# A transformer block's first FFN layer by seven half products: GpSimd's add moved behind the last product, a Relu moved one step later, and the residual rows added in the second pair step

## The chip, the cores and the metric

The kernel runs on one core of one Trainium2 chip. The time is the device time of an execution in microseconds (us); for the kernel before it is the median of three runs. The engines are called PE (TensorE: matmuls, into PSUM), DVE (VectorE), ACT (ScalarE), POOL (GpSimd) and SP (SyncE, which only issues DMAs here). Each engine works through its own queue of instructions in order.

## The reference, cut to what matters

Eight sequences (batches) of 1024 rows with 256 features go through one block: normalise, self-attention, gated residual, normalise, a two-layer FFN with Relu, gated residual. All is float32.

```python
h = _layernorm(x, axis=-1) * (1 + ca) + sa
x = x + ga * _L0_attn_ref(h, L0_attn_w_lhs, L0_attn_w_rhs)   # softmax(lhs @ rhs^T) @ h
h = _layernorm(x, axis=-1) * (1 + cb) + sb
x = x + gb * _L0_ffn_ref(h, L0_ffn_W1, L0_ffn_b1, L0_ffn_W2, L0_ffn_b2)

def _L0_ffn_ref(hidden_states, W1, b1, W2, b2):
    h = jax.nn.relu(jnp.einsum('bsh,hi->bsi', hidden_states, W1) + b1)    # 256 -> 1024
    return jnp.einsum('bsi,ih->bsh', h, W2) + b2                          # 1024 -> 256
```

## The kernel before, in words

**Steps.** A batch b has eight steps i, one for each tile of 128 rows of its attention. A step makes the scores of the row tile two steps ahead (`direct`, L372: PE, then a copy by ACT to SBUF), the maximum of a row (`row_max`), its subtraction (`subtract`, L439, DVE), the exponent (`exponent`, L451, ACT) and the product of weights and values (`product`, L456: 16 matmuls of 257 columns on PE; then `product_out` on DVE). Scores are symmetric in their shape: `mirror` (L393) makes the other half by a block transpose on DVE and a trip through DRAM on SP's queue.

**The FFN of an earlier half batch runs in the same steps.** A half batch (group g, 512 rows) of batch b-1 needs four steps: in the first two (i = 0, 1 for one group, 4, 5 for the other; the code's `first`) the first layer, two *pairs* of 128 hidden columns each, so pairs c = 0, 1 in step 0 or 4 and c = 2, 3 in step 1 or 5. In the other two the second layer: `y_first` (L655) and `y_second` (L677).

**A pair.** `pair_products` (L581) and `pair_last` (L625) make the columns c and c+4 for both 256-row halves with seven half-size products in place of eight, and sums around them. Six products go to the PSUM tiles pa, pb and pc; ACT copies pa to `kept` (L598). `pair_sums` (L607) then adds: DVE's L611 and L614 make `u`, POOL's L617 adds the second half of `kept` to both parts of `u` and writes the second halves of both column blocks of f, DVE's L620 and L623 write the first halves. `pair_last` issues the seventh product into pa, and DVE's L630 adds it to what POOL wrote. `pair_relu` (L632) applies the Relu on ACT (L634, L635) and `pair_turn` (L639) makes the sums ft that the second layer reads (POOL, L644 to L647; `ft[:, 1]`, called ft1 here, by L645).

**The second layer** takes f (both blocks, all four pairs) in ya and yb, then ft1 and ft0 in the second halves of ya and yb, then the rest in `y_second`. Its result goes through a transpose in DRAM; the read comes back as Y behind a mirror's read on SP's queue (`read_back`). `y_add` (L716, POOL's L721, two instructions of 512 elements) adds it to x, and `y_out` stores x.

**Buffers.** Four PSUM tiles (`ps_a`) serve pa, pb, pc, the attention's product and ya to yd; two (`ps_s`) serve the scores. `kept` has two buffers, Y, f and ft have one each.

**Order.** Instructions stay in the order in which the program writes them, engine by engine (`pin`, L61). The main loop's body (L988 to L1136) is that order. In a pair step it reads: products of the first pair, its sums, the turn of the pair before, mirror, last product, subtract, products of the second pair, Relu of the first, exponent, sums of the second, turn of the first, `y_add` (in steps 0 and 4, by `back`), row_max, last product and Relu of the second. After that come `subtract(extra)`, `turns` (in step 5 `prepare_turn`, L319, which makes lT on DVE, L335, and rT on ACT, L339, for the next batch's scores), `norms` (in step 1 a memset and a power on POOL, in step 5 a power), the last turn, and the attention's product. Behind the loop the last batch's FFN follows without attention, with a plain second layer (`second`, L749).

Of the kernel before, what the change touches and what calls it, by code (L numbers as in the profile page):

```python
# [10 lines left out]
F32 = mybir.dt.float32  # L11
AF = mybir.ActivationFunctionType
ALU = mybir.AluOpType
# [3 lines left out]
P = 128  # L17
# [5 lines left out]
def adaln_block_kernel(  # L23
# [13 lines left out]
    nc = tc.nc  # L37
# [5 lines left out]
    HALF = 512  # L43
    TH = HALF // P
    H2 = HALF // 2
    NH = NI // 2
# [6 lines left out]
    work = ctx.enter_context(tc.tile_pool(name="work", bufs=3))  # L53
# [113 lines left out]
    b1_col = lambda i: cols[:, i : i + 1]  # L167
# [111 lines left out]
    def read_back():  # L279
        while reads:  # L280
            reads.pop(0)()
# [111 lines left out]
    def mirror(b, i):  # L393
        if i == NT - 1:
            return
        n = NT - 1 - i
        if b == 0:
            mirror_first(i)
            return
        T = two.tile([P, NV, NT * V], F32, tag="T", name=f"Tm_{b}_{i}")  # L400
        T = T.rearrange("p b m -> p (b m)")[:, : NV * n * V].rearrange(
            "p (b m) -> p b m", b=NV
        )
        nc.vector.transpose(  # L404
            T.rearrange("p b (j v) -> p b j v", v=V),
            sc_t[b][:, i + 1 :, :, i, :].rearrange("p j b v -> p b j v"),
        )
        move(
            sc_t[b][:, i, :, i + 1 :, :].rearrange("p a j v -> p a (j v)"), T, n * V,
            f"m{b}_{i}",  # L410
        )
# [39 lines left out]
    def exponent(b, i):  # L451
        nc.scalar.activation(pT_t[b, i], pT_t[b, i], AF.Exp)  # L452
# [122 lines left out]
    lo, hi = slice(0, H2), slice(H2, HALF)  # L575
    pairs = {}

    def mm(out, lhsT, rhs):
        nc.tensor.matmul(out, lhsT=lhsT, rhs=rhs, start=True, stop=True)  # L579

    def pair_products(b, g, c, between=None):  # L581

        if c == 0:
            ffn["f"] = two.tile([P, NI, HALF], F32, tag="f", name=f"f_{b}_{g}", bufs=1)
            if b < B - 1:
                ffn["ft"] = two.tile([P, 3, NH, H2], F32, tag="ft", name=f"ft_{b}_{g}", bufs=1)
        hT, hs = ffn["hT", g]
        n = ts(c, P)
        s1, a22 = (w1[:, k, ds((c + NH) * P, P)] for k in range(2))

        pool, tag = (ps_s, "s") if b == B - 1 else (ps_a, "a")
        pa = ps_a.tile([P, HALF], F32, tag="a", name=f"pa_{b}_{g}_{c}")
        pb = pool.tile([P, HALF], F32, tag=tag, name=f"pb_{b}_{g}_{c}")
        pc = ps_a.tile([P, HALF], F32, tag="a", name=f"pc_{b}_{g}_{c}")
        mm(pa[:, lo], w1[:, 0, n], hT[:, 0, lo])
        mm(pa[:, hi], s1, hs[:, 0])
        kept = work.tile([P, HALF], F32, tag="kept", name=f"kept_{b}_{g}_{c}", bufs=2)
        nc.scalar.copy(kept, pa)  # L598
        if between:
            between()  # L600
        mm(pb[:, lo], w1s[:, 0, n], hs[:, 1])
        mm(pb[:, hi], w1s[:, 1, n], hs[:, 2])
        mm(pc[:, lo], w1[:, 1, n], hT[:, 1, lo])
        mm(pc[:, hi], a22, hT[:, 0, hi])
        pairs[c] = pa, pb, pc, kept

    def pair_sums(b, g, c):  # L607
        pa, pb, pc, kept = pairs[c]
        f = ffn["f"]
        u = work.tile([P, 2, H2], F32, tag="u", name=f"u_{b}_{g}_{c}", bufs=2)  # L610
        nc.vector.scalar_tensor_tensor(  # L611
            u[:, 0], pb[:, lo], b1_col(c), kept[:, lo], ALU.add, ALU.add
        )
        nc.vector.scalar_tensor_tensor(  # L614
            u[:, 1], pb[:, hi], b1_step[:, c : c + 1], u[:, 0], ALU.add, ALU.add
        )
        nc.gpsimd.tensor_tensor(  # L617
            f[:, c::NH, hi], u, kept[:, None, hi].to_broadcast([P, 2, H2]), ALU.add
        )
        nc.vector.scalar_tensor_tensor(  # L620
            f[:, c, lo], pc[:, lo], b1_col(c), kept[:, lo], ALU.add, ALU.add
        )
        nc.vector.tensor_tensor(f[:, c + NH, lo], pc[:, hi], u[:, 1], ALU.add)  # L623

    def pair_last(b, g, c):  # L625

        pa = pairs.pop(c)[0]
        f = ffn["f"]
        mm(pa[:, lo], w1s[:, 2, ts(c, P)], ffn["hT", g][0][:, 1, hi])
        nc.vector.tensor_tensor(f[:, c, hi], pa[:, lo], f[:, c, hi], ALU.add)  # L630

    def pair_relu(c):  # L632
        f = ffn["f"]
        nc.scalar.activation(f[:, c, :], f[:, c, :], AF.Relu)  # L634
        nc.scalar.activation(f[:, c + NH, :], f[:, c + NH, :], AF.Relu)  # L635
# [3 lines left out]
    def pair_turn(c):  # L639


        f, ft = ffn["f"], ffn["ft"]
        add = nc.gpsimd.tensor_tensor
        add(ft[:, 0, c], f[:, c + NH, hi], f[:, c, hi], ALU.subtract)  # L644
        add(ft[:, 1, c], ft[:, 0, c], f[:, c, lo], ALU.add)  # L645
        add(ft[:, 2, c], ft[:, 1, c], f[:, c + NH, lo], ALU.subtract)
        add(f[:, c, hi], f[:, c, hi], f[:, c, lo], ALU.subtract)  # L647
# [68 lines left out]
    def y_add(b, g, q):  # L716

        read_back()
        x2 = x_t[b, g][:, ts(q, 2), :].rearrange("p t (h b u) -> p (t h) b u", h=2, u=V)
        y = ffn["rows", b, g].rearrange("p t h b u -> p (t h) b u")[:, ts(q, 4)]  # L720
        nc.gpsimd.tensor_tensor(x2, x2, y, ALU.add)  # L721
# [100 lines left out]
    b1_step = const.tile([P, NH], F32, name="b1_step")  # L822
# [105 lines left out]
    def turns(b, i):  # L928

        if b > 0 and i == 2:  # L930
            ffn_turn(b - 1, 1)
        if 0 < b < B - 1:
            if i == 3:
                prepare_turn(b + 1, 0)
            elif i == 5:
                prepare_turn(b + 1, 1)
        if i == (7 if b < B - 1 else 6):
            ffn_turn(b, 0)
# [45 lines left out]
    def weights(b, i):  # L984
        subtract(b, i)
        exponent(b, i)
# [3 lines left out]
    for b in range(B):  # L990
        for i in range(NT):
# [4 lines left out]
            fb, fg = b - 1, i // TH  # L996
            first = b > 0 and i % TH < 2
            c = i % TH * 2
# [48 lines left out]
            if first:  # L1047

                ub, ug = (b - 1, 0) if i >= TH else (b - 2, 1)
                back = i % TH == 0 and ub >= 0  # L1050
                pair_products(fb, fg, c, turn_max)
                if (b, i) == (1, 0):
                    weights(*late)
                    late = None
                pair_sums(fb, fg, c)
                if c > 0:
                    pair_turn(c - 1)
                if ahead:
                    mirror(*ahead)
                pair_last(fb, fg, c)  # L1060
                if i == 4 and b + 1 < B:
                    prepare_blocks(b + 1, 1)
                    xg_times(b + 1, 1)
                if late:
                    subtract(*late)
                pair_products(fb, fg, c + 1, (lambda: max_turn(*extra)) if extra else None)
                pair_relu(c)
                if late:
                    exponent(*late)
                middle(b, i)  # L1070
                pair_sums(fb, fg, c + 1)
                pair_turn(c)
                if back:
                    for q in range(2):
                        y_add(ub, ug, q)
                if ahead and ahead != extra:
                    row_max(*ahead)
                pair_last(fb, fg, c + 1)
                pair_relu(c + 1)
            else:  # L1080
                half = i % TH - 2
                if i == 3 and b + 1 < B:
                    prepare_stats(b + 1, 1)
                if not ahead:

                    product(b, i)
                    product_out(b, i)
                    if i == NT - 1:
                        ffn_stats(b, 1)
                (y_second if half else y_first)(fb, fg, turn_max)  # L1090
                if ahead:
                    mirror(*ahead)
                spare()
                early(b, i)
                if late:
                    weights(*late)
                middle(b, i)
                if i == 2 and b + 1 < B:
                    load_x(b + 1, 1)
                if i == 3 and b + 1 < B:  # L1100
                    prepare_norm(b + 1, 1)
                    x_plus(b + 1, 1)
                spare()
                if ahead:
                    row_max(*ahead)
                if half:
                    y_second_sums(fb)
                else:
                    y_first_sums()
                spare()  # L1110
            if extra:
                subtract(*extra)
            turns(b, i)
            norms(b, i)
            if extra:
                exponent(*extra)
# [24 lines left out]
    b = B - 1  # L1141
# [73 lines left out]
```

## Time and profile before

| what | value |
|---|---|
| three timed runs | 791.08, 792.75, 793.41 us; median 792.75 |
| the profiled execution's own time | 792.76 us |
| its span, first to last instruction | 790.9 us |
| mean granted clock of PE | 0.998 |
| POOL's longest waits | for DVE's L558 at L567 107.7 us in 15, for L614 at L617 101.3 us in 35 |
| ACT's waits at Relu L634 for DVE's L630 | 76.6 us in 56 |
| DVE's waits at L630 for POOL's L617 | 29.9 us in 28 |
| POOL's waits at L721 for the read of Y | 20.4 us in 8, the longest 8.4 |
| one batch in steady state | 94.0 us, for instance from 236.39 to 330.29 in step 5's product |

In a row of a timeline the first number is the start in us from the first instruction, the second the stretch that the row covers; then engine, line, operation, output and inputs, and the count of instructions. A bracket at the end is the idle time of the engine before it, and what ended that. In a row of the list of waits the numbers are the total in us, how often, and the longest. Idle time of an engine other than PE costs nothing by itself.

### The profile page before, as it was taken

Reading aid. Unit: us, or ns where it says so; the run is one execution under the profiler, and the core shown is the slowest. Engines: PE = TensorE matmul, PEld = TensorE weight load, DVE = VectorE, ACT = ScalarE, POOL = GpSimd, SP = SyncE. Lnnn points to the kernel's source line nnn. Section 1 sums busy time; section 2 is a strip of 40 time slices with the busy share of each in tenths; the row PEclk is TensorE's granted clock in tenths of the full one; section 3 lists DMA queues with packets and bytes.
Section 4 is the critical chain, followed back from the end, with each engine's and each line's share of the span. In section 5 each row is a group of like instructions: output and inputs, shape, how many; then the busy total and the mean of one; then the engine's idle time right before and its main releaser. Section 6 shows DMA issues by size and latency. Waiting matters only on the chain.

```text
span 790.9 us, 10632 instructions
## 1 busy us (share of the span) xinstructions
PE 771.9 (98%) x3374; PEld 619.8 (78%) x3374; DVE 564.2 (71%) x1212; ACT 346.9 (44%) x581; POOL 461.6 (58%) x573
## 2 busy tenths in 40 slices
PE   8999999999999999999999998999999999999997
PEld 4676888778887888778887886878888778888886
DVE  6696889658786778857888567885789658574632
ACT  4463535425444454435445344452535425242511
POOL 1365665927657385745759347493665927357631
PEclk9999999999999999999999999999999999999999
DMA  5323344355444354344533544335444345142220
GB/s 188 121 74 116 109 123 126 104 143 166 121 111 135 111 170 132 115 144 119 157 97 110 172 122 126 98 114 172 129 148 120 96 126 166 34 123 85 80 81 27
DMA packets 106192, 95.14 MB, mean 120 GB/s; under 512 B 29684, under 2 KB 98832, under 8 KB 106136
## 3 DMA queue, kind: packets, MB, share of 16 engines
q1 hardware_dynamic: 98392, 85.81, 36.6%
q10 hardware_dynamic: 7744, 8.65, 3.7%
q8 instruction: 27, 0.44, 0.2%
q14 instruction: 29, 0.24, 0.1%
HBM read 50.62 MB, written 43.81 MB: 119 GB/s over the span
## 4 chain that ended last, share of the span: by engine, by line
PE 72%; DVE 10%; POOL 9%; issue 5%; ACT 2%; DMA 1%; SPq 0%; DVEq 0%; POOLq 0%
PE po L464 20%; PE psc L381 13%; PE yc L651 6%; PE ya L651 6%; PE yb L651 6%; PE pa L579 6%; POOL f L617 5%; PE pb L579 4%; PE pc L579 3%; PE yd L651 3%; DVE pT L443 2%; POOL x L721 2%; PE py L756 2%; DVE u L614 2%; DVE u L611 1%
## 5 line engine op out<-in xcount | busy, mean ns | idle before, releaser
L464 PE MATMUL po<-xg,pT 128*128 128x257 f32 x1024 | 235.6, 383 | 5.2 <-DVE f L630 5.2
L464 PEld LDWEIGHTS po<-xg,pT 128*128 128x128 f32 x1024 | 194.4, 191 | 36.4 <-DVE f L630 8.4
L617 POOL TENSOR_TENSOR f<-u,kept 128x512 f32<-128x512 f32 x64 | 81.3, 1271 | 101.5 <-DVE u L614 101.3
L381 PE MATMUL psc<-rT,lT 128*128 128x512 f32 (+3 forms) x384 | 135.9, 488 | 3.9 <-ACT rT L339 3.9
L388 ACT COPY sc<-psc 128x512 f32<-128x512 f32 (+3 forms) x96 | 45.2, 474 | 147.3 <-PE psc L381 147.3
L381 PEld LDWEIGHTS psc<-rT,lT 128*128 128x128 f32 x384 | 68.2, 190 | 44.7 <-issue 22.5
L452 ACT ACTIVATE pT<-pT 128x1024 f32<-128x1024 f32 x64 | 67.7, 1058 | 54.5 <-DVE pT L443 54.5
L443 DVE TENSOR_TENSOR pT<-sc,pm 128x1024 f32<-128x1024 f32 x64 | 77.2, 1207 | 16.7 <-PE pm L436 16.7
L431 DVE TENSOR_REDUCE m<-sc 128x1 f32<-128x1024 f32 x64 | 77.4, 1210 | 0.6
L598 ACT COPY kept<-pa 128x512 f32<-128x512 f32 x64 | 37.5, 585 | 87.0 <-PE pa L579 87.0
L567 POOL TENSOR_TENSOR hs<-hT 128x256 f32<-128x256 f32 x16 | 11.7, 730 | 107.7 <-DVE hT L558 107.7
L634 ACT ACTIVATE f<-f 128x512 f32<-128x512 f32 x64 | 40.5, 632 | 77.6 <-DVE f L630 76.6
L579 PE MATMUL pb<-hs,w1s 128*128 128x256 f32 x256 | 65.9, 380 | 0.7 <-POOL hs L569 0.7
L579 PE MATMUL pc<-hT,w 128*128 128x256 f32 x256 | 65.7, 379 | 0.0
L611 DVE SCALAR_TENSOR_TENSOR u<-pb,cols,kept 128x256 f32<-128x256 f32 x64 | 30.6, 479 | 40.0 <-PE pb L579 39.1
L579 PEld LDWEIGHTS pc<-hT,w 128*128 128x128 f32 x256 | 48.6, 190 | 6.6
L630 DVE TENSOR_TENSOR f<-pa,f 128x256 f32<-128x256 f32 x64 | 27.0, 421 | 36.5 <-POOL f L617 29.9
L495 POOL TENSOR_TENSOR x<-x,rows 128x256 f32<-128x256 f32 x64 | 45.5, 739 | 12.1 <-ACT rows L857 12.1
L579 PEld LDWEIGHTS pb<-hs,w1s 128*128 128x128 f32 x256 | 45.8, 190 | 8.6 <-POOL hs L569 1.1
L651 PE MATMUL yc<-f,w2s 128*128 128x256 f32 x224 | 52.1, 379 | 0.0
L651 PEld LDWEIGHTS yc<-f,w2s 128*128 128x128 f32 x224 | 41.5, 190 | 10.2 <-issue 2.9
L404 DVE STREAM_TRANSPOSE Tm<-sc 128x896 f32<-128x896 f32 (+6 forms) x49 | 34.7, 708 | 19.1 <-ACT sc L388 18.3
(135 smaller groups left out, 1411.2 us busy)
## 6 DMA issues: line engine op xcount, KB each, us to landing
D_f<-T_f SPq DMA_DIRECT2D x60, 128.0 KB, 2.8
X_f<-D_f SPq DMA_DIRECT2D x15, 512.0 KB, 3.5
D_a<-T_a SPq DMA_DIRECT2D x56, 128.0 KB, 3.3
D_y<-T_y SPq DMA_DIRECT2D x56, 128.0 KB, 2.3
Y<-D_y SPq DMA_DIRECT2D x14, 512.0 KB, 3.9
out_dram<-x SPq DMA_DIRECT2D x14, 512.0 KB, 4.0
X_a<-D_a SPq DMA_DIRECT2D x13, 512.0 KB, 3.2
x<-in_L_attn_x_dram ACTq DMA_DIRECT2D x12, 512.0 KB, 4.0
```

The costliest lines, as they stand in the source:

```text
L381: nc.tensor.matmul(psc[:, : hi - lo], lhsT=lT_t[b, i // TH][:, k, ts(i % TH, P)], rhs=rT_t[b, n][:, k, lo - n * HALF : HALF], start=(k == ...
L388: nc.scalar.copy(score_row(b, i)[:, lo // V : hi // V, :], psc[:, : hi - lo].rearrange("p (n v) -> p n v", v=V),)
L431: nc.vector.tensor_reduce(m, score_row(b, i), AX.XY, ALU.max)
L443: nc.vector.tensor_tensor(pT.rearrange("p j (a v) -> p j a v", v=V), score_columns(b, i), pm[:, :P].rearrange("p (j a v) -> p j a v", j=1, ...
L452: nc.scalar.activation(pT_t[b, i], pT_t[b, i], AF.Exp)
L464: nc.tensor.matmul(po[:, : D + 1], lhsT=pT[:, t, :], rhs=xg_t[b][:, t, 0 : D + 1], start=(t == 0), stop=(t == NT - 1),)
L495: queue.append(lambda: nc.gpsimd.tensor_tensor(out, in0, row, op))
L579: nc.tensor.matmul(out, lhsT=lhsT, rhs=rhs, start=True, stop=True)
L611: nc.vector.scalar_tensor_tensor(u[:, 0], pb[:, lo], b1_col(c), kept[:, lo], ALU.add, ALU.add)
L617: nc.gpsimd.tensor_tensor(f[:, c::NH, hi], u, kept[:, None, hi].to_broadcast([P, 2, H2]), ALU.add)
L634: nc.scalar.activation(f[:, c, :], f[:, c, :], AF.Relu)
L651: nc.tensor.matmul(out, lhsT=lhs(c), rhs=rhs(c), start=(c == 0), stop=(c == NH - 1))
```

## The change

In `pair_sums` DVE writes u (half as large) and, in place of its second part, the second half of block c+4 of f itself; POOL's add is gone from there. `pair_last` adds the seventh product to u and writes the second half of block c; POOL's add of `kept` follows it, in place on both blocks of f. `kept` gets a third buffer. In the main loop the Relu of a second pair moves from the end of steps 0 and 4 to behind the first products of steps 1 and 5; the turn of the pair before follows the last product instead of the sums; the second pair's last product comes ahead of `row_max` and of the first pair's turn. `y_add`, and with it `y_out`, moves from steps 0 and 4 to steps 1 and 5, between the turn of pair 1 and the last product of pair 3. In step 5 `turns` is called ahead of the last Relu instead of behind it. The code behind the loop is unchanged, but calls the changed functions.

```diff
-        kept = work.tile([P, HALF], F32, tag="kept", name=f"kept_{b}_{g}_{c}", bufs=2)
+        kept = work.tile([P, HALF], F32, tag="kept", name=f"kept_{b}_{g}_{c}", bufs=3)
...
     def pair_sums(b, g, c):
-        u = work.tile([P, 2, H2], F32, tag="u", name=f"u_{b}_{g}_{c}", bufs=2)
+        u = work.tile([P, H2], F32, tag="u", name=f"u_{b}_{g}_{c}", bufs=2)
+        pairs[c] = pa, kept, u
+        far = f[:, c + NH, hi]
         nc.vector.scalar_tensor_tensor(
-            u[:, 0], pb[:, lo], b1_col(c), kept[:, lo], ALU.add, ALU.add
+            u, pb[:, lo], b1_col(c), kept[:, lo], ALU.add, ALU.add
         )
         nc.vector.scalar_tensor_tensor(
-            u[:, 1], pb[:, hi], b1_step[:, c : c + 1], u[:, 0], ALU.add, ALU.add
-        )
-        nc.gpsimd.tensor_tensor(
-            f[:, c::NH, hi], u, kept[:, None, hi].to_broadcast([P, 2, H2]), ALU.add
+            far, pb[:, hi], b1_step[:, c : c + 1], u, ALU.add, ALU.add
         )
...
-        nc.vector.tensor_tensor(f[:, c + NH, lo], pc[:, hi], u[:, 1], ALU.add)
+        nc.vector.tensor_tensor(f[:, c + NH, lo], pc[:, hi], far, ALU.add)
...
     def pair_last(b, g, c):
-        pa = pairs.pop(c)[0]
+        pa, kept, u = pairs.pop(c)
         mm(pa[:, lo], w1s[:, 2, ts(c, P)], ffn["hT", g][0][:, 1, hi])
-        nc.vector.tensor_tensor(f[:, c, hi], pa[:, lo], f[:, c, hi], ALU.add)
+        nc.vector.tensor_tensor(f[:, c, hi], pa[:, lo], u, ALU.add)
+        nc.gpsimd.tensor_tensor(
+            f[:, c::NH, hi],
+            f[:, c::NH, hi],
+            kept[:, None, hi].to_broadcast([P, 2, H2]),
+            ALU.add,
+        )
...
-                back = i % TH == 0 and ub >= 0
+                back = i % TH == 1 and ub >= 0
                 pair_products(fb, fg, c, turn_max)
...
+                if c > 0:
+                    pair_relu(c - 1)
                 pair_sums(fb, fg, c)
-                if c > 0:
-                    pair_turn(c - 1)
                 if ahead:
                     mirror(*ahead)
                 pair_last(fb, fg, c)
+                if c > 0:
+                    pair_turn(c - 1)
+                if back:
+                    for q in range(2):
+                        y_add(ub, ug, q)
...
                 pair_sums(fb, fg, c + 1)
-                pair_turn(c)
-                if back:
-                    for q in range(2):
-                        y_add(ub, ug, q)
+                pair_last(fb, fg, c + 1)
                 if ahead and ahead != extra:
                     row_max(*ahead)
-                pair_last(fb, fg, c + 1)
-                pair_relu(c + 1)
+                pair_turn(c)
+                if i == 5:
+                    turns(b, i)
+                if c > 0:
+                    pair_relu(c + 1)
...
-            turns(b, i)
+            if i != 5:
+                turns(b, i)
```

## The prediction

> **What bounds the kernel now.** I read the page's busy times first, then the list of who waited for whom, cut to TensorE (PE), and then the timelines of single engines in the two places it points at. The page settles the kind of kernel:
>
> ```profile
> PE 771.9 (98%) x3374; PEld 619.8 (78%) x3374; DVE 564.2 (71%) x1212; ACT 346.9 (44%) x581; POOL 461.6 (58%) x573
> L617 POOL TENSOR_TENSOR f<-u,kept 128x512 f32<-128x512 f32 x64 | 81.3, 1271 | 101.5 <-DVE u L614 101.3
> ```
>
> PE is busy 98% of a 790.9 us span. The change adds and removes no matmul, so a time can change only through PE's pauses. In the list of waits those inside the loop have two names:
>
> ```profile
> PE po L464 <- DVE f L630: 5.2, 8, 2.6
> PE psc L381 <- ACT rT L339: 3.9, 6, 0.7
> ```
>
> The reader is to see that 8 and 6 are about one per batch (b = 1 to 7), plus one outlier of 2.6 us. The ends of matmuls are modelled, so I size the pauses from start to start, in the timeline of PE around step 5 of batch 3:
>
> ```profile
> 329.38 0.59 PE L579 MATMUL pa<-hT,w1s 128*128 128x256 f32 x2
> 330.29 3.73 PE L464 MATMUL po<-xg,pT 128*128 128x257 f32 x16 [0.32 <-DVE f L630]
> 333.86 1.88 PE L381 MATMUL psc<-rT,lT 128*128 128x512 f32 x4
> 336.39 1.98 PE L381 MATMUL psc<-rT,lT 128*128 128x512 f32 x4 [0.65 <-ACT rT L339]
> ```
>
> Two 256-wide matmuls take 0.43 us from start to start and four 512-wide 1.73, as neighbouring rows show. So the product could start at 329.81 and starts 0.48 later; the second score half could start at 335.59 and starts 0.80 later: 1.28 us per batch, in batches 1 to 6. Batch 7, without the score part, loses 0.88 (711.15 against 710.27). The outlier is in batch 5, step 1:
>
> ```profile
> 474.43 0.59 PE L579 MATMUL pa<-hT,w1s 128*128 128x256 f32 x2
> 477.60 5.42 PE L464 MATMUL po<-xg,pT 128*128 128x257 f32 x16 [2.58 <-DVE f L630]
> 482.86 1.88 PE L381 MATMUL psc<-rT,lT 128*128 128x512 f32 x4
> ```
>
> Starting at 474.86, with 3.47 us for a product, the scores would come at 478.33; they come 4.5 later: 2.74 of pause and 1.8 because the granted clock of the stretch 478.28 to 481.69 was 0.50. Its cause is y_add (L721): it waited 4.95 us for the read of Y, and L617 and L630 stood behind it. Recoverable in the loop: 6 x 1.28 + 0.88 + 4.5 = 13.1 us.
>
> [...] L617 of the third pair starts at 328.51, at the end of y_add, though its input was ready at 327.37. All that follows rests on it. [...] PE was busy 0.83 of 3.41 us before the drop. [...] L647 takes 0.91 instead of 0.73 us at 336.25, beside the tensor_scalar of L335.
>
> **The change part by part.**
>
> *GpSimd's add moves behind the seventh product.* Same operation, 512 elements in place; the nearest row is y_add's, in place too: 1.27 us, as L617. So 64 for 64, nothing gained in busy time. VectorE's L630 no longer waits for GpSimd (29.9 us in 28 waits, idle time). But the Relu now waits for GpSimd, about 1.4 us later (0.13 to start, 1.27, 0.04 to the release).
>
> *Step 5 (prepare_turn ahead of the last Relu, y_add no longer in step 4).* VectorE is no longer stopped at L630: from the blocks' transposes it runs 0.57 earlier, and as the Relu of pair 1 leaves the way of the score copy, L630 of pair 2 ends at about 327.84, where the product needs it at 329.81: that stall goes. GpSimd adds pair 2 at 327.97; Relu 2 ends at 330.4, the exponent at 331.4, then ACT does rT (2 x 0.75) until 333, where the scores need it at 335.0. Second stall gone: -6 x 1.28 - 0.88 = -8.6 us. What is late next is GpSimd: add 327.97, turn of pair 1 329.19 (a turn takes 3.0), y_add 332.2 (2.46), add of pair 3 334.66, turn of pair 2 335.88, power 338.85, turn of pair 3 339.83, whose second output, ft1, ends at 341.4. PE, now earlier, wants it at 341.49 (336.73 for the end of the scores, 3.46 for ya and yb, 1.30 for six matmuls). That is no margin; with 0.18 lost beside L335, 0 to 0.4 us per batch. I take 0.2: +1.2.
>
> *Step 1 gets y_add.* This is the part that decides. Before, GpSimd and PE in batch 3:
>
> ```profile
> 281.77 2.51 POOL L721 TENSOR_TENSOR x<-x,Y 128x512 f32<-128x512 f32 x2 [1.31 <-DMA Y<-D_y]
> 284.23 1.28 POOL L617 TENSOR_TENSOR f<-u,kept 128x512 f32<-128x512 f32 x1
> 288.46 1.27 POOL L617 TENSOR_TENSOR f<-u,kept 128x512 f32<-128x512 f32 x1
> 294.67 0.73 POOL L645 TENSOR_TENSOR ft<-ft,f 128x256 f32<-128x256 f32 x1
> ```
>
> ```profile
> 292.08 1.89 PE L651 MATMUL ya<-f,w 128*128 128x256 f32 x8
> 295.64 1.89 PE L651 MATMUL ya<-ft,w2s 128*128 128x256 f32 x8
> ```
>
> From 284.23 GpSimd has no idle time until 295.40, when ft1 of pair 3 is ready (the L645 row). PE uses it in the seventh of the second row's eight matmuls, at 295.64 + 6 x 0.216 = 296.94: 1.54 us to spare. After: the add of pair 2 must wait for L630 (VectorE ends L623 and the mirror's transpose at 285.17, L630 at 285.59), so it starts at 285.72, 1.49 later. Then turn 1 (286.94), y_add (289.95), add 3 (292.41), turn 2 (293.64), memset and power (296.6), turn 3 (297.8): ft1 at 299.35. PE waits 2.43 us; 1.0 of it is spent earlier, at 293.38, where ya wants Relu 3, which cannot end before 292.41 + 1.27 + 0.67 = 294.35. Nothing covers it: only four score matmuls (1.73 us) lie between the pairs and y here, half as many as after step 5. Batches 2 to 6: +12.2. Batch 7 has no memset and power (1.21): +1.2. Batch 1 has no y_add here and just fits.
>
> *The read of Y.* y_add one step later, some 10 us after the read's issue, never waits for it: -4.5, and the DMA issue itself stays where it is on SP's queue (behind the mirror's read). The output store moves a step too; its wait on SP ends at 292.4, ahead of SP's next issue at 294.64. The load of x that reuses its tile stands in ACT's queue a step later (297.16 before); the store lands about 4.0 us after 292.5, so it holds nothing.
>
> *ACT at step 0.* Relu 0 is 1.4 later, so exponent, ffn_norm (ends 279.54) and the transposes behind it on VectorE (280.88) are too. product_out ends at 282.1, ahead of the pair sums that PE releases at 282.85. Cost nothing; 0.7 us is the cover.
>
> *The third kept buffer*, as the add reads kept later: no time.
>
> *The tail.* ACT's order is Relu of pair c-1, then the copy of pair c+1; the last product of pair 3 overwrites what that copy reads. With the Relus 1.4 later, the last group's copy of pair 3 (771.30 before) comes behind L630 of pair 1 (ends 770.2), its add (771.6) and its Relu (772.8), ends at 773.4, and PE, due at 772.53, waits 0.9. In the first group such a wait ends in one that exists anyway (hs behind y_add, 759.5), of which 0.2 is added: +1.1 (0.3 to 1.5).
>
> **Sum:** -8.6 - 4.5 + 1.2 + 13.4 + 1.1 = +2.6 us on the profiled execution's 792.76 (span 790.9 and 1.9 around it); the median of the runs, 792.75, is the same number. Forecast 795.3 us.
>
> **The rivals.**
> - *Not slower: GpSimd's queue catches up.* One mechanism, step 1: if ft1 is ready before PE wants it, the 13.4 fall away: 781.9. It decides below a chain of 11.2 us from 285.72; I make it 13.6 from this trace's own pitches, so all of y_add would have to run beside something. For it: a delay of VectorE or PE elsewhere would give slack. Half of the chain's excess gone gives 788.6.
> - *Half clock.* The two pauses, 1.0 and 1.4 us, could bring the 0.50 clock as in batch 5: 1.5 more in five batches, 802.8. Against it: the pause at step 5 leaves 2.76 of 3.41 us busy, the stretch 24.31 to 27.72 2.73, both at clock 1.00; at 2.0 of 3.4 the trace shows nothing.
> - *The late read was only in the profiled run.* Then 4.5 are not to be had: 799.8. Against it: profiled time and median agree.
>
> **How the numbers follow.** A measurement of this kernel tells about 0.3% from no change, 2.4 us: 790.4 to 795.1. Forecast case 0.60 (its own range 793.0 to 798.0: 0.02 faster, 0.25 same, 0.33 slower), catching up 0.18 (faster), half clock 0.10 and no late read 0.12 (slower). Faster 0.20, same 0.25, slower 0.55. The range 787 to 801 leaves out the full catching up and the half clock.
>
> **What would show it.** Right: a new PE wait at L651 for ACT's Relu and for GpSimd's ft1, about 2.4 us a batch, at step 2; no waits at L464 and L381 in step 5; y_add never waiting for Y; PE waiting before the last product in the tail. Wrong: no wait at L651, or GpSimd idle between the add of pair 2 and the turn of pair 3 in step 1.

## The result and the profile after

The changed kernel takes 794.37 us (median of 20 runs, 794.10 to 797.08). The kernel before, run beside it, takes 793.29 us (20 runs, 791.08 to 795.07). The ratio is 1.0023, interval 1.0013 to 1.0032: 0.2% slower, within what was set as no change that can be told. The profiled execution took 794.97 us (span 793.1) against 792.76 (span 790.9). The forecast was 795.3. The medians differ by 1.1 us, where 2.6 were forecast, and the case "no change that can be told" had been given a chance of 0.25, "slower" 0.55.

Behind this small number stand pauses of TensorE that went, 15.7 us in all, and others that came, 17.4 us (the sums are taken apart below). From the page of the kernel after, the busy times and two groups of instructions (in the new file the four sums are L613 to L622, GpSimd's add is L631, the Relus L640 and L641, the turn L650 to L653, y's products L657, y_add L727):

```profile
PE 772.3 (97%) x3374; PEld 618.2 (78%) x3374; DVE 568.1 (72%) x1212; ACT 340.3 (43%) x581; POOL 462.5 (58%) x573
L631 POOL TENSOR_TENSOR f<-f,kept 128x512 f32<-128x512 f32 x64 | 81.3, 1270 | 152.3 <-DVE f L630 118.2
L640 ACT ACTIVATE f<-f 128x512 f32<-128x512 f32 x64 | 40.4, 631 | 105.0 <-POOL f L631 105.0
```

The add costs what it did (81.3 us, 1270 ns each); only the directions of the waits have turned. GpSimd now waits for VectorE's L630, and the Relu for GpSimd. The list of who waited for whom, cut to TensorE, shows what that means for the engine that sets the time (total us, times, longest):

```profile
PE ya L657 <- POOL ft L651: 5.0, 5, 1.0
PE ya L657 <- ACT f L640: 4.6, 6, 0.8
...
PE pa L579 <- ACT kept L598: 1.3, 2, 0.7
...
PE pb L579 <- DVE f L616: 0.3, 1, 0.3
```

The two old names are gone: po (the tile of the attention's product) at L464, and psc (that of the scores) at L381 for rT. Two new ones stand at y's first products (tile ya): 5 waits for ft1 are batches 2 to 6, the 6 for the Relu have batch 7 as well. TensorE's timeline at the end of step 1 and in step 2 of batch 3 shows them:

```profile
291.19 1.88 PE L381 MATMUL psc<-rT,lT 128*128 128x512 f32 x4
292.91 1.46 PE L657 MATMUL ya<-f,w 128*128 128x256 f32 x6
295.13 0.70 PE L657 MATMUL ya<-f,w 128*128 128x256 f32 x2 [0.76 <-ACT f L640]
...
297.50 1.46 PE L657 MATMUL ya<-ft,w2s 128*128 128x256 f32 x6
299.97 0.70 PE L657 MATMUL ya<-ft,w2s 128*128 128x256 f32 x2 [1.01 <-POOL ft L651]
```

Six matmuls at a pitch of 0.216 us take 1.30. So the seventh was due at 294.21 and 298.80; it starts 0.92 and 1.17 later, and the matmul behind it a further 0.10 late each time: 2.29 us a batch. GpSimd's timeline of the same stretch shows why:

```profile
286.47 1.27 POOL L631 TENSOR_TENSOR f<-f,kept 128x512 f32<-128x512 f32 x1 [3.92 <-ACT kept L598]
287.70 0.73 POOL L650 TENSOR_TENSOR ft<-f 128x256 f32<-128x256 f32 x1
...
290.69 2.49 POOL L727 TENSOR_TENSOR x<-x,Y 128x512 f32<-128x512 f32 x2
293.15 1.26 POOL L631 TENSOR_TENSOR f<-f,kept 128x512 f32<-128x512 f32 x1
294.37 0.73 POOL L650 TENSOR_TENSOR ft<-f 128x256 f32<-128x256 f32 x1
...
299.19 0.73 POOL L651 TENSOR_TENSOR ft<-ft,f 128x256 f32<-128x256 f32 x1
```

Only the first line has an idle time before it. Its bracket names the copy of kept, but L630, which it also needs, ended at 286.33. From 286.47 on the engine is busy to 299.92, where ft1 of pair 3 is ready; 2.46 us of that are y_add. In step 5 of the same batch there is no pause left on TensorE, and in step 6 a short one:

```profile
332.51 0.59 PE L579 MATMUL pa<-hT,w1s 128*128 128x256 f32 x2
332.95 3.63 PE L464 MATMUL po<-xg,pT 128*128 128x257 f32 x16
336.41 3.60 PE L381 MATMUL psc<-rT,lT 128*128 128x512 f32 x8
339.85 1.89 PE L657 MATMUL ya<-f,w 128*128 128x256 f32 x8
...
343.30 2.25 PE L657 MATMUL ya<-ft,w2s 128*128 128x256 f32 x8
```

The product follows the last pair product at the plain pitch (0.44 us for two), and all eight score matmuls run in one row, where four had waited for rT before. In step 6 the row that reads ft takes 2.25 us, where one without a pause takes 1.89: the short wait for ft1 there, some 0.37 us in batches 1 to 6.

### The profile page after: what moved, and what is told of

Its sections match the earlier page's. It is cut to its first block, busy times and chain, and to the rows that moved or that the text cites. A ratio compares the mean times of both kernels' runs of the same rounds, so it can differ in the third digit from the quotient of the medians.

```text
span 793.1 us, 10553 instructions
## 1 busy us (share of the span) xinstructions
PE 772.3 (97%) x3374; PEld 618.2 (78%) x3374; DVE 568.1 (72%) x1212; ACT 340.3 (43%) x581; POOL 462.5 (58%) x573
## 4 chain that ended last, share of the span: by engine, by line
PE 69%; POOL 19%; DVE 6%; issue 2%; ACT 2%; DMA 1%; SPq 0%; POOLq 0%; DVEq 0%; ACTq 0%
PE po L464 21%; PE psc L381 11%; PE pa L579 7%; PE yc L657 6%; POOL f L631 4%; PE pb L579 4%; PE pc L579 4%; POOL x L727 4%; PE yb L657 4%; PE py L762 4%; POOL ft L651 3%; PE yd L657 3%; POOL ft L650 3%; POOL f L653 2%; PE ya L657 2%
## 5 line engine op out<-in xcount | busy, mean ns | idle before, releaser
L464 PE MATMUL po<-xg,pT 128*128 128x257 f32 x1024 | 233.0, 380 | 0.0
L464 PEld LDWEIGHTS po<-xg,pT 128*128 128x128 f32 x1024 | 193.9, 190 | 27.9 <-issue 1.0
L631 POOL TENSOR_TENSOR f<-f,kept 128x512 f32<-128x512 f32 x64 | 81.3, 1270 | 152.3 <-DVE f L630 118.2
L381 PE MATMUL psc<-rT,lT 128*128 128x512 f32 (+3 forms) x384 | 134.5, 486 | 0.4 <-ACT sc L388 0.4
L381 PEld LDWEIGHTS psc<-rT,lT 128*128 128x128 f32 x384 | 68.6, 190 | 39.3 <-issue 27.7
L640 ACT ACTIVATE f<-f 128x512 f32<-128x512 f32 x64 | 40.4, 631 | 105.0 <-POOL f L631 105.0
L443 DVE TENSOR_TENSOR pT<-sc,pm 128x1024 f32<-128x1024 f32 x64 | 77.1, 1205 | 6.7 <-PE pm L436 6.7
L613 DVE SCALAR_TENSOR_TENSOR u<-pb,cols,kept 128x256 f32<-128x256 f32 x64 | 30.6, 477 | 32.5 <-PE pb L579 31.0
L657 PE MATMUL yc<-f,w2s 128*128 128x256 f32 x224 | 52.1, 379 | 0.0
L657 PEld LDWEIGHTS yc<-f,w2s 128*128 128x128 f32 x224 | 41.5, 190 | 10.2 <-issue 2.9
L652 POOL TENSOR_TENSOR ft<-ft,f 128x256 f32<-128x256 f32 x56 | 40.8, 729 | 4.4
```

Source lines behind the costliest of these rows:

```text
L381: nc.tensor.matmul(psc[:, : hi - lo], lhsT=lT_t[b, i // TH][:, k, ts(i % TH, P)], rhs=rT_t[b, n][:, k, lo - n * HALF : HALF], start=(k == ...
L443: nc.vector.tensor_tensor(pT.rearrange("p j (a v) -> p j a v", v=V), score_columns(b, i), pm[:, :P].rearrange("p (j a v) -> p j a v", j=1, ...
L464: nc.tensor.matmul(po[:, : D + 1], lhsT=pT[:, t, :], rhs=xg_t[b][:, t, 0 : D + 1], start=(t == 0), stop=(t == NT - 1),)
L631: nc.gpsimd.tensor_tensor(f[:, c::NH, hi], f[:, c::NH, hi], kept[:, None, hi].to_broadcast([P, 2, H2]), ALU.add,)
L657: nc.tensor.matmul(out, lhsT=lhs(c), rhs=rhs(c), start=(c == 0), stop=(c == NH - 1))
```

## The experiments

The theory: the change is three things that can be taken apart. GpSimd's add behind the seventh product frees VectorE at L630; the early turns of step 5 (prepare_turn and the multiply by the exponent ahead of the last Relu) keep rT ahead of the scores; y_add in the second pair step lengthens GpSimd's chain to ft1 and takes back what the first two give. The main rival: the Relus, which now wait for GpSimd, cost the time, wherever y_add stands. Every ratio below is against the kernel before in the same job, with its interval.

### y_add back in the first pair step

```diff
-                back = i % TH == 1 and ub >= 0
+                back = i % TH == 0 and ub >= 0
...
-                if back:
-                    for q in range(2):
-                        y_add(ub, ug, q)
...
                 pair_turn(c)
+                if back:
+                    for q in range(2):
+                        y_add(ub, ug, q)
```

> The changed kernel with one part undone: y's rows are added by GpSimd in the first pair step again (steps 0 and 4, behind the turn of that step's first pair), the rest stays. Theory (y_add in the second pair step is what lengthens GpSimd's chain to ft1): the waits of TensorE at y_first go, 2.29 us in batches 2 to 6 and 1.26 in batch 7, and the 0.37 at step 6 in batches 1 to 6, together 14.9 us: about 780 to 782 us against the changed kernel's 794.4, the upper end where the read of Y is late. Rival (the Relus behind GpSimd's moved add are what costs, with or without y_add in that step): the waits for Relu 3 and ft1 stay, 793 to 795 us. Second rival (the late read of Y costs as much as before when y_add is early): a pause of 2 to 4.5 us in a batch, 782 to 785 us.

Measured: 780.03 us (779.5 to 782.34), ratio 0.9839 (0.9816 to 0.9863). GpSimd and TensorE in step 1 and 2 of batch 3:

```profile
282.51 1.28 POOL L631 TENSOR_TENSOR f<-f,kept 128x512 f32<-128x512 f32 x1 [1.14 <-ACT kept L598]
...
286.75 1.26 POOL L631 TENSOR_TENSOR f<-f,kept 128x512 f32<-128x512 f32 x1
...
292.80 0.73 POOL L651 TENSOR_TENSOR ft<-ft,f 128x256 f32<-128x256 f32 x1
```

```profile
287.23 1.88 PE L381 MATMUL psc<-rT,lT 128*128 128x512 f32 x4
288.94 1.89 PE L657 MATMUL ya<-f,w 128*128 128x256 f32 x8
...
292.51 1.89 PE L657 MATMUL ya<-ft,w2s 128*128 128x256 f32 x8
```

The chain from the add of pair 2 to the end of ft1 is now 11.02 us (282.51 to 293.53), against 13.45 in the changed kernel. The seventh matmul of ya's second half is due at 293.81, 0.28 after ft1: both rows run whole. All waits at y_first fall away but one of 0.36 us (batch 5). The Relus stand behind GpSimd's add here too, so the rival is out. The store of x moves back with y_add in this run; the run with half of y_add, below, leaves it in the second step. The second rival is not settled. The read of Y was late again in batch 5, but less than before (y_add waited 2.06 us, against 4.95), and it cost 0.46 us. In the traces of three kernels with the moved add and this y_add in step 0 (this one, the next, and that of the tail), waits of 2.06, 2.88 and 2.35 us cost 0.46, 1.29 and 0.74 at y_first, in each 1.6 less than the wait. So freeing L630 does not cure a late read; it is then paid at ft1. Why it came less late is not shown. This kernel is faster than the two of the forecast.

### Only the second group's rows back

```diff
-                back = i % TH == 1 and ub >= 0
+                back = i in (0, 5) and ub >= 0
...
-                if back:
+                if back and i == 5:
...
                 pair_turn(c)
+                if back and i == 0:
+                    for q in range(2):
+                        y_add(ub, ug, q)
```

> The changed kernel with the rows of y's second group alone added in step 0 again; the first group's stay in step 5. Theory: only the waits at step 2 go (2.29 us in batches 2 to 6, 1.26 in batch 7: 12.7 us), the 0.37 us of batches 1 to 6 at step 6 stay: about 782 us, some 2 us behind the kernel that undoes both. Rival (Relus behind the add): 793 to 795 us.

Measured: 782.62 us (781.46 to 783.45), ratio 0.9865 (0.9845 to 0.9886). The waits at step 2 are gone, the 0.37 us at step 6 are there in batches 1 to 6, and the late read of batch 5 (2.88 us) leaves 1.29. So the two places of y_add are priced apart: some 12 us in step 1, and 2.2 (six times 0.37) in step 5.

### Half of y_add in each step

```diff
-                back = i % TH == 1 and ub >= 0
+                back = i % TH < 2 and ub >= 0
...
-                if back:
-                    for q in range(2):
-                        y_add(ub, ug, q)
+                if back and i % TH == 1:
+                    y_add(ub, ug, 1)
...
                 pair_turn(c)
+                if back and i % TH == 0:
+                    y_add(ub, ug, 0)
...
-            if first and back:
+            if first and back and i % TH == 1:
                 y_out(ub, ug)
```

> The changed kernel with half of y's rows added in the first pair step (steps 0 and 4) and half in the second (1 and 5), the store behind the second half: 1.23 us of GpSimd instead of 2.46 in the chain to ft1. Theory (each us of GpSimd's queue ahead of ft1 counts in full once the slack is used up): of the 2.29 us in batches 2 to 6 at step 2 about 1.1 is left, the wait for Relu 3 gone and the one for ft1 kept; batch 7 and step 6 have no wait: 780.0 + 5 x 1.1 = 785 to 786 us. Rival (a threshold: half of it fits beside other work): 780 to 781 us. Second rival (not the length but the place of the instruction counts, as it stands between add 2 and add 3): 790 us or more.

Measured: 785.06 us (784.69 to 786.43), ratio 0.9897 (0.9866 to 0.9928). TensorE in step 2 of batch 3:

```profile
291.86 1.89 PE L657 MATMUL ya<-f,w 128*128 128x256 f32 x8
...
295.42 1.46 PE L657 MATMUL ya<-ft,w2s 128*128 128x256 f32 x6
297.71 0.70 PE L657 MATMUL ya<-ft,w2s 128*128 128x256 f32 x2 [0.83 <-POOL ft L651]
```

The wait for Relu 3 is gone and the one for ft1 is 1.00 + 0.10 us, five times: 5.5 us over the kernel with none, where 5.0 were measured. Taking 1.23 us off GpSimd's chain takes 1.19 off TensorE's pause. The store stands in the second step here, so it is GpSimd's time that counts and not the store's place. Of y_add's 2.46 us hardly anything is free: only the 0.28 us of margin that are left without it.

### The early turns of step 5 undone

```diff
                 pair_turn(c)
-                if i == 5:
-                    turns(b, i)
...
-            if i != 5:
-                turns(b, i)
+            turns(b, i)
```

> The changed kernel with prepare_turn and the multiply by the exponent of step 5 (turns) behind the last Relu again, as in all other steps. Theory (that early place is what keeps rT ahead of the scores, since the Relu now waits for GpSimd's add of pair 3, which stands behind y_add): rT comes at about 338 us in batch 3 where the scores want it at 335, a wait at L381 of 2.5 to 3 us in batches 1 to 6, against 0.37 us at step 6 that it covers: about 808 us. Rival (the place of turns does not matter, the step-5 pauses went because VectorE no longer waits for GpSimd at L630): 794 to 796 us.

Measured: 822.82 us in one run. The right sign and place; the size is off. TensorE in step 5 of batch 3, and below it the granted clock of three stretches there (PEclk):

```profile
345.09 1.88 PE L381 MATMUL psc<-rT,lT 128*128 128x512 f32 x4
349.95 3.49 PE L381 MATMUL psc<-rT,lT 128*128 128x512 f32 x4 [2.98 <-ACT rT L339]
```

```profile
core 0: us, PE busy (x) PEld busy (x) DVE busy (x) ACT busy (x) POOL busy (x), PEclk, DMA share, GB/s
345.00:350.00 5.00, 2.02 (x7) 0.69 (x5) 2.98 (x6) 1.96 (x4) 4.84 (x6) 0.96 0.31 107
350.00:353.60 3.60, 3.60 (x6) 1.75 (x7) 0.00 (x0) 2.14 (x4) 3.44 (x6) 0.58 0.00 0
353.60:358.00 4.40, 4.40 (x22) 3.88 (x21) 2.69 (x3) 2.90 (x6) 4.40 (x7) 1.00 0.40 104
```

The scores wait 3.14 us, a little more than the 2.5 to 3 expected. Behind this pause the granted clock is 0.58 from 350.00 to 353.60 (the same four score matmuls take 3.49 instead of 1.88 us), and the mean of the execution is 0.985, which the expectation had left out. At half clock that mean stands for some 25 us (an estimate: 2 x 0.015 x 821.0 us of span), about 4 for each of the six pauses if all of it lies there. The waits at step 2 stand unchanged beside it. The early turns are no detail: without them the change is a loss of nearly 30 us.

### Both undone

```diff
-                back = i % TH == 1 and ub >= 0
+                back = i % TH == 0 and ub >= 0
...
                 pair_turn(c)
-                if i == 5:
-                    turns(b, i)
+                if back:
+                    for q in range(2):
+                        y_add(ub, ug, q)
```

> The changed kernel with y's rows added in the first pair step and, beside that, the turns of step 5 behind the last Relu again. Theory (add 3 comes 2.46 us earlier without y_add ahead of it, so of the 3.14 us that the late turns cost with y_add in step 5 about 0.7 is left): 0.7 us in batches 1 to 6, 784 to 785 us against 780.0. Rival (without y_add in step 5 the early turns are worth nothing): 780 us. Second rival (they cost the same 3 us without y_add): 800 us or more.

Measured: 792.38 us (20 runs, 790.18 to 796.12), ratio 0.9995 (0.9982 to 1.0008). The expectation was wrong in size: the scores wait 1.74 us in batches 1 to 6, not 0.7. GpSimd in step 5 of batch 3, and the line of VectorE that makes the input of the first add:

```profile
327.54 2.50 POOL L727 TENSOR_TENSOR x<-x,Y 128x512 f32<-128x512 f32 x2
330.00 1.28 POOL L631 TENSOR_TENSOR f<-f,kept 128x512 f32<-128x512 f32 x1
...
334.41 1.44 POOL L631 TENSOR_TENSOR f<-f,kept 128x512 f32<-128x512 f32 x1
```

```profile
328.39 0.41 DVE L630 TENSOR_TENSOR f<-pa,u 128x256 f32<-128x256 f32 x1
```

L630 of pair 2 ends at 328.80, but y_add holds GpSimd until 330.0. So moving y_add to step 4 does not take 2.46 us out of the chain to the add of pair 3. There it delays the add of pair 2 by 1.1 us, and with it all that follows, so that only 2.46 - 1.06 = 1.40 us are gained: 3.14 - 1.40 = 1.74.

### The parts alone, on the kernel before

y_add alone in the second pair step (steps 1 and 5), the rest of the old order:

```diff
-                back = i % TH == 0 and ub >= 0
+                back = i % TH == 1 and ub >= 0
...
                 pair_last(fb, fg, c)
+                if back:
+                    for q in range(2):
+                        y_add(ub, ug, q)
...
                 pair_turn(c)
-                if back:
-                    for q in range(2):
-                        y_add(ub, ug, q)
```

> The kernel before with one part of the change alone: y's rows added in the second pair step (steps 1 and 5), behind the turn of the pair before. Theory: the late read of Y no longer stops L630, but GpSimd's chain in the second pair step is 2.46 us longer: in step 1 a wait at y_first of about 0.9 us (1.5 us of slack was there) in batches 2 to 6, in step 5 the wait for rT at L381 grows from 0.8 to 2 to 3 us in batches 1 to 6: 798 to 806 us against the 793.3 of the kernel before. Rival (the slack at y_first and the scores take it up): 788 to 793 us, the late read's share saved.

Measured: 804.34 us (803.65 to 806.12), ratio 1.0143 (1.0116 to 1.017). TensorE's waits of this kernel:

```profile
PE psc L381 <- ACT rT L339: 16.1, 6, 2.7
PE ya L651 <- POOL ft L645: 2.8, 5, 0.6
```

The two waits are those of the theory (2.85 and 0.72 us from start to start). They tell that y_add in the second step is a loss in the old order too, though it no longer waited for Y in the loop. The list has no po any more: in batch 1 the product starts at 141.81, 0.43 us after the last pair product at 141.38. So this edit alone ends the first stall of step 5, although VectorE waits longer at L630 for GpSimd than before (49.1 us in 30 waits, against 29.9 in 28). What delayed the product was y_add ahead of the add of pair 2, and moving either of the two is enough.

The turns alone, ahead of the last Relu of step 5:

```diff
                 pair_last(fb, fg, c + 1)
+                if i == 5:
+                    turns(b, i)
                 pair_relu(c + 1)
...
-            turns(b, i)
+            if b == 0 or i != 5:
+                turns(b, i)
```

> The kernel before with one part of the change alone: in step 5 prepare_turn and the multiply by the exponent (turns) stand ahead of the last Relu. Theory: ACT makes rT 1.3 us earlier, the 0.80 us wait of the scores for rT in batches 1 to 6 goes (4.9 us), the 0.48 us wait of po for L630 and the late read of Y stay: 787 to 790 us against 793.2. Rival (rT is late because VectorE, which stops at L630 for GpSimd, makes its inputs late): 792 to 794 us.

Measured: 785.2 us (784.11 to 788.11), ratio 0.9909 (0.9882 to 0.9935): more than expected. ScalarE in step 5 of batch 1:

```profile
144.23 1.50 ACT L339 ACTIVATE rT<-X_a,sides 128x512 f32<-128x512 f32 x2
146.35 0.63 ACT L634 ACTIVATE f<-f 128x512 f32<-128x512 f32 x1 [0.62 <-DVE f L630]
```

rT now runs while the Relu of pair 3 has no input yet, and the scores wait in no batch (5.5 us gone with the 0.10 after each). The po waits stay. The rest of the gain in this trace, about 3.0 us, comes from a late read of batch 5 that cost 2.0 instead of 4.5 and from the tail, where TensorE didn't wait for hs (1.25 before), less 0.8 for longer po waits in batches 3 and 7. How late that read comes differs between executions (its pause was 2.74 us in the trace of before and 1.92 here, with y_add in the same place), so it isn't shown to be a gain of this edit. Why the tail's wait for hs (inputs of the first products, made by GpSimd) went is not shown either. Against this kernel, the one with y_add back (780.03 us) has in addition the moved add with its order of calls: that is worth some 5 us, once the turns are early and y_add stands in the first step.

GpSimd's add alone, in place behind the seventh product, in the old order of the calls (with u of half the size and the third kept buffer):

```diff
         nc.vector.tensor_tensor(f[:, c, hi], pa[:, lo], u, ALU.add)
+        nc.gpsimd.tensor_tensor(
+            f[:, c::NH, hi], f[:, c::NH, hi],
+            kept[:, None, hi].to_broadcast([P, 2, H2]), ALU.add,
+        )
```

> The kernel before with one part of the change alone: GpSimd's add in place behind the seventh product (with u in one half and the third kept buffer), in the old order: the turn and y_add of a step stand ahead of that step's second add, and the Relu stands where it stood. Theory (GpSimd's queue is first in, first out, so the add must be moved ahead of the turns with it): Relu 1 waits behind turn 0 and y_add, turn 1 behind Relu 1, add 2 behind turn 1, and so on; by the pitches of the trace Relu 3 ends about 4 us after TensorE wants it at y_first in step 2 and about as much in step 6: 4 to 6 us in 11 places, 835 to 860 us. Rival (the add's place matters only through VectorE's L630, which no longer waits): the po waits of 0.48 us go, 788 to 793 us.

Measured: 880.23 us in one run. One place in batch 1, on ScalarE and on TensorE:

```profile
143.69 0.63 ACT L640 ACTIVATE f<-f 128x512 f32<-128x512 f32 x1 [7.48 <-POOL f L631]
...
144.88 0.59 ACT L598 COPY kept<-pa 128x512 f32<-128x512 f32 x1
```

```profile
145.53 1.22 PE L579 MATMUL pa<-hT,w1s 128*128 128x256 f32 x2 [4.30 <-ACT kept L598]
```

The sign is the theory's and the rival is out, but the wait isn't where it was expected. It is not y that waits: the Relu waits 7.48 us for an add that stands behind y_add in GpSimd's queue (y_add from 139.95, the add from 142.39 to 143.65), the copy of the next pair's kept (144.88) stands behind that Relu in ScalarE's queue, and the seventh product, which overwrites what the copy reads, waits for it: 63.5 us in 16 waits. A part of it is the read of Y, for which y_add itself waited 1.54 us here and 35.0 us in 14 waits in all. The order of the calls in the change (sums, last product and add, then the turn of the pair before; the Relu after the next pair's copy) is what makes the moved add possible; its parts were not tried one by one.

### The tail

The kernel with y_add back, and in the tail each pair's Relus one product step later, behind the copy that held up the last product:

```diff
             pair_products(b, g, c)
+            if c > 1:
+                pair_relu(c - 2)
...
                 pair_last(b, g, c - 1)
-                pair_relu(c - 1)
...
         pair_last(b, g, NH - 1)
+        pair_relu(NH - 2)
         pair_relu(NH - 1)
```

> The changed kernel with y's rows added in the first pair step, as in the run that undid this part, and in the tail each pair's Relus one product step later, behind the copy of kept that TensorE waits for. Theory (ACT's queue in the tail: the copy of pair 3 stands behind Relu 1, which waits for GpSimd's add): the two waits before the last product, 0.86 and 0.73 us, go: about 778.3 us where the kernel without it had 780.0. Rival (the later Relus of pairs 2 and 3 delay the second layer): 779.5 to 781 us.

Measured: 780.05 us (779.07 to 780.78), ratio 0.9835 (0.9814 to 0.9857): no gain. The second layer's first products in the last group:

```profile
759.76 1.89 PE L762 MATMUL py<-w2g,f 128*128 128x256 f32 x8
762.08 4.24 PE L762 MATMUL py<-w2g,f 128*128 128x256 f32 x18 [0.44 <-ACT f L640]
```

The waits before the last product are gone, and py waits for a Relu instead: 0.86 and 0.60 us in the two groups, where 0.86 and 0.73 went. Those Relus wait for GpSimd's add in turn, so another chain ended just behind the copy's wait.

## Why the forecast held

Between the kernels that keep the moved add, only two edits differ; the four times (us) show how they act on each other:

| | turns of step 5 early | turns late |
|---|---|---|
| y_add in the first pair step | 780.03 | 792.38 |
| y_add in the second (the change) | 794.37 | 822.82 (one run) |

y_add's place costs 14.3 us with the early turns and about 30 without. Now term by term, each counted in the two profiled executions as TensorE's lateness from start to start, the 0.10 us after a pause with it:

| step of the prediction | forecast | measured |
|---|---|---|
| pauses of step 5 go | -8.6 | -10.0 |
| late read of Y in batch 5 goes | -4.5 | -4.5 |
| step 1 to 2: chain to Relu 3 and ft1 | +13.4 | +12.7 |
| step 5 to 6: ft1 without margin | +1.2 | +2.2 |
| step 5 of batch 7 | 0 | +0.5 |
| tail | +1.1 | +0.7 |
| sum | +2.6 | +1.6 |

The profiled executions differ by 2.2 us; the rest lies before the first changed step, where the pauses came to 11.3 and 12.1 us (11.1 to 12.9 in the traces of the experiments).

*Step 5.* Right: both stalls went. The forecast left out the 0.10 us that follow each pause: 13 times, 1.3 us. That the wait for rT needs the early turns is shown by the turns alone and by the two runs with the turns late. The wait of po had two cures in this change: it went with y_add moved alone, and also in the two kernels that have the moved add and y_add in the first step (780.03 and 792.38 us). So the freed L630 would have been enough, but was not needed.

*Step 1 to 2.* Right, and the step that decides: 2.29 us against 2.43 a batch (2.41 by its own figures, 299.35 less 296.94). Batch 7 came out at 1.26 against 1.2, but by another wait. The sum had ft1 late by 1.2 there; in the trace the Relu of pair 3 is late by 0.92, and ft1 by 0.14. The rival "GpSimd's queue catches up" needed y_add to run beside something; the halved y_add shows that it runs beside nothing.

*Step 5 to 6.* The forecast's bound of 0 to 0.4 us held, with 0.37 near its upper end.

*Step 5 of batch 7.* Here the forecast left something out: it found that Relu 0, some 1.4 us later, costs nothing because of 0.7 us of cover, but looked at step 0 alone. ScalarE in step 4 of batch 7, where it also makes X_f, the normalised rows, changed kernel and kernel before:

```profile
702.03 0.63 ACT L640 ACTIVATE f<-f 128x512 f32<-128x512 f32 x1 [1.04 <-POOL f L631]
...
704.03 2.06 ACT L511 ACTIVATE X_f<-x,rs_f,rb 128x256 f32<-128x256 f32 x4
```

```profile
698.93 0.63 ACT L634 ACTIVATE f<-f 128x512 f32<-128x512 f32 x1 [0.18 <-DVE f L630]
...
701.02 2.08 ACT L511 ACTIVATE X_f<-x,rs_f,rb 128x256 f32<-128x256 f32 x4
```

The changed kernel is 2.23 us later at this place by TensorE's rows, so the Relu slips by 0.87 and X_f by 0.78. The transposes behind X_f and the sums behind them on VectorE slip with them, and the next pair's second product waits 0.44 for L616. In step 0, and in step 4 of the other batches, the cover held.

*The tail.* The two waits for the copy of kept came as forecast, with 0.86 and 0.72 us. The hs wait of the kernel before, assumed to stay, went. In the loop y_add never waited for Y, as forecast; in the tail, where its place is unchanged, it waited 5.4 us once.

*The late read.* In the pair of profiled executions it is worth the 4.5 us of the forecast. The rival, that only the profiled run had it, has the clocks against it: of 25 runs of the kernel before in one job, four were granted 0.999 or more and took 790.5 to 791.8 us, the other 21 had 0.995 to 0.998 and took 791.5 to 795.0. One stretch of 3.41 us at 0.50, as in the trace, takes 0.002 off the mean of a run (0.5 x 3.41 / 790.9), so such stretches are likely in most of them (an estimate). That one came from this read was seen in the one trace alone, and low clocks occur elsewhere too (the profiled execution of the halved y_add was granted 0.997, with no wait of TensorE above 1.5 us in its list), so the read's share in the medians stays open; they differ by 1.1 us, the profiled executions by 2.2.

*Half clock.* The rival of 802.8 us did not occur: the granted clock of the profiled execution is 1.000, and of the 20 runs none is below 0.997. The seven that took 795.5 us or more had 0.997 to 0.999, so single low stretches are likely in them; where is not on record.

*The sum.* That it came within 1 us is in part luck: the steps missed by -1.4, -0.7, +1.0, +0.5 and -0.4 us, and the misses cancel in part.

## What to carry to other kernels

Before work is moved on an engine that takes its queue in order, add up its chain to the next consumer's due time. Where the chain has no idle time and the slack is smaller than the moved work, all that exceeds the slack is paid, here 2.3 us of a 2.46 us addition in five batches. A change of several parts whose sum is nothing deserves a run with each part undone: here one part out of three cost 14 us and the other two, together, earned 13, and leaving that part out gives 780.0 us, the best kernel of the case. A wait that goes is worth its length only if no other chain ends just behind it, as the tail shows.

## What the runs showed of the hardware

- Half clock and pauses of TensorE. In the trace of before the granted clock was 0.50 for 3.41 us (478.28 to 481.69), from 0.68 us after the end of the pause of 2.74 us, and 1.00 after all others in batches 1 to 7 (0.47 to 0.88 us). The changed kernel, with pauses up to 1.17 us there, was granted 1.000 in its profiled execution. That of y_add alone on the kernel before, with six waits of 2.85 us for rT, had 0.993: behind the wait of batch 1 the clock was 0.61 from 149.9 to 154.3, behind that of batch 2 it was 1.00 from 247.9 to 252.0. With the turns late (six of 3.14 us) it was 0.985, with GpSimd's add alone (16 waits for kept, 63.5 us in all, the longest 7.1) 0.955. So the low clock came with long pauses, but no single length decides: the kernel with six pauses of 1.74 us had granted clocks from 1.000 to 0.995 in its 20 runs. The runs at 1.000 took 790.2 to 792.5 us, those at 0.995 some 796. That the busy share of a stretch of 3.41 us decides, as the forecast's shares of it suppose, is not shown.
- After a pause the second matmul, too, starts a further 0.10 us late: 0.32 us after the first where the plain pitch is 0.22, and 0.53 for 0.43 with 512 columns. The traces of before and after show this for all pauses of 0.22 to 2.74 us in batches 1 to 7 and in the tail. That is small, but there are some 20 of them here.
- Work stood behind earlier instructions of its engine, though its own input was ready. On GpSimd, with both parts undone, the add of pair 2 started at 330.00, at the end of y_add, with its input ready at 328.80. On VectorE, in the trace of before, L443 started at 330.15, behind L630, which had waited 1.72 us; the matmul that makes its pm had ended at 327.81. On ScalarE, with GpSimd's add alone, the copy of kept at 144.88 stood behind the Relu that waited 7.48 us, and TensorE had been idle since 141.23.
- Beside VectorE's L335 some of GpSimd's instructions took longer. In batches 1 to 6 the last row of a turn (L647 before, L653 after) took 0.90 to 0.92 us there (median 0.73), and in the changed kernel y_add's first half 1.45 (median 1.27); the row before (L646, L652), of which at least 0.49 us lay beside L335 too, took its 0.73. What makes the difference is not shown.
